# Eight PSUM banks, cut differently: four pairs, or two pairs and four single banks

## The chip, the cores and the metric

The kernel runs on one core of a Trainium2 chip. The metric is device time in microseconds (us), the median of several runs. In the text PE is the matrix engine (TensorE), ACT the activation engine (ScalarE), DVE the vector engine (VectorE), POOL is GpSimd and SP the engine that issues most transfers. PSUM is the memory into which PE writes; ACT and DVE empty it. It has eight banks of 512 float32 values for each of 128 partitions, and one matmul writes into one bank.

## The reference

Eight images of 8 channels and 256 x 256 pixels pass through a grouped Fourier neural operator (4 groups of 2 channels), with a residual, and then through a 3 x 3 dilation with a residual. Everything is float32.

```python
# layer 0, on the normalised x, per group: 2 channels and 2 grid planes -> 10 channels
h = _gconv1x1(h, fc0_w, fc0_b)
for i in range(4):
    h1 = _spectral_conv(h, sp_w1[i], sp_w2[i])   # FFT, 24 x 12 modes kept, mixed, FFT back
    h2 = _gconv1x1(h, w_w[i], w_b[i])
    h = h1 + h2
    if i < 3:
        h = _gswish(h, betas[i])
h = _gswish(_gconv1x1(h, fc1_w, fc1_b), betas[3])   # 10 -> 128 channels per group
x = x + _gconv1x1(h, fc2_w, fc2_b)                  # 128 -> 2 channels per group
# layer 1
x = x + dilate3x3(_gn(x))
```

## The kernel before: the parts concerned

The four Fourier layers of image b ("layers") and the fc1/fc2 part of image b - 1 ("head") are interleaved: the program puts single steps of the head between pieces of the layers. The instructions of PE, ACT and DVE stand in a fixed order that the program gives. The first image's layers have no head beside them, and the last image's head has no layers beside it.

Every PSUM tile comes from one ring of four pairs of banks. A tile that needs only one bank takes a pair and leaves half of it unused. A taker waits until the tile that had its place four takings earlier has been read.

```python
def ps_z(name):
    return ps.tile([128, 2, 512], F32, tag="z", bufs=4, name=name)

def ps_a(name):
    return ps_z(name)[:, 0, :]
```

Four places fill four banks at once, with one matmul per bank from each of four row groups of PE. Two of them, with the copy of the Fourier rows between:

```python
def copy_2(i, dst, src):
    if i % 2:
        nc.scalar.activation(dst, src, AF.Identity)
    else:
        nc.vector.tensor_copy(dst, src)

def turn(c):                       # DVE, after burst(c): two transpositions of h
    # ... for i in range(2): of h[:, c, 2 * i : 2 * i + 2]

def transform(k):                  # rows to frequencies, two chunks of h
    pair = [ps_z(f"p_d_{b}_{l}_{k}_{i}") for i in range(2)]
    for v in range(8):
        for q in range(NQ):
            mm(pair[q // 2][part(v % 4), q % 2, : 240 * n], fw8[part(q), v, :],
               t[part(q), :, :, v, : NBLK * WID], start=v < 4, stop=v >= 4)
    for i in range(2):
        copy_2(i, e[:, 2 * i : 2 * i + 2], pair[i][:, :, : 240 * n])

def gather(k):                     # sums the four parts of a transform, one bank
    p = ps_a(f"p_u_{b}_{l}_{k}")
    # ... four matmuls, a copy to zt by DVE

def burst(c):                      # one chunk of the next h: 1x1 convolution and rows back
    pair = [ps_z(f"p_z_{b}_{l}_{c}_{i}") for i in range(2)]
    for f in range(NQ):
        for q in range(NQ):
            o = pair[q // 2][part(f), q % 2, :]
            # ... mm(o, weights, h[:, c, f], start=True, stop=False)
    for s in range(2):
        for q in range(NQ):
            mm(pair[q // 2][:, q % 2, HW * s : HW * (s + 1)],
               zt[part(q), 2 * c + s].rearrange("p f o -> p (f o)"), binv[part(q), :],
               start=False, stop=s == 1)
    for i in range(2):
        dst = h[:, c, 2 * i : 2 * i + 2, :]
        if l < 3:
            nc.scalar.activation(dst, pair[i], AF.Silu)
        else:
            nc.scalar.activation(dst, pair[i], AF.Identity, bias=bias3)
```

The head has 128 steps an image. Each step calls `first`; each even one calls `second` before it.

```python
def first(n):                      # fc1 of one piece of 512 pixels, four groups
    act = sb.tile([128, G, 512], F32, tag="act", bufs=4, name=f"act_{b}_{n}")
    pair = [ps_z(f"p_fc1_{b}_{n}_{i}") for i in range(2)]
    for g in range(G):
        mm(pair[g // 2][:, g % 2, :], w1[part(g), blk, :], hs[k][part(g), :], start=True, stop=True)
    for i in range(2):
        nc.scalar.activation(act[:, 2 * i : 2 * i + 2, :], pair[i], AF.Silu)

def second(n):                     # fc2 of two pieces, into one bank
    y, acc = box["y"], ps_a(f"p_fc2_{b}_{n}")
    for i in range(2):
        act = acts.pop(n + i)
        for g in range(G):
            mm(acc[part(g), :], w2[:, g, 15 - rb - i : 47 - rb - i], act[:, g, :],
               start=i == 0, stop=i == 1)
    # ... DVE adds acc to y

# the head's loop
if n % 2 == 0 and n > 3:
    second(n - 4)
first(n)
```

Other takers of PSUM: `rows_of` (tile `p_g`, a pair each, five per layer and image, emptied by DVE), the transpositions of x (`p_xt`, a pair each), and single banks for sums, `p_b`, `p_f` and the like. In layers 0 to 2, two chunks of a layer run in the order burst, second, first, transform, burst, gather, first; in layer 3, a chunk is burst, first, second, first.

Of the kernel before, what the change touches and what calls it, by code (L numbers as in the profile page):

```python
# [10 lines left out]
F32 = mybir.dt.float32  # L11
AF = mybir.ActivationFunctionType
# [6 lines left out]
HW = 256  # L19
# [25 lines left out]
def fno_dilate_kernel(ctx: ExitStack, tc: tile.TileContext, a: dict, out: bass.AP):  # L45
    nc = tc.nc
    mm = nc.tensor.matmul
# [4 lines left out]
    ps = ctx.enter_context(tc.tile_pool(name="ps", bufs=2, space=PSUM))  # L52
# [1 line left out]


    def ps_z(name):
        return ps.tile([128, 2, 512], F32, tag="z", bufs=4, name=name)

    def ps_a(name):
        return ps_z(name)[:, 0, :]  # L60

    def part(i):
        return slice(32 * i, 32 * i + 32)
# [10 lines left out]
    def load(name, shape, eng=nc.gpsimd):  # L74
        t = const.tile(list(shape), F32, tag=f"c_{name}", name=f"c_{name}")
        eng.dma_start(t, a[name])
        return t
# [9 lines left out]
    fw8 = load("fw8", (128, 8, 32), nc.sync)  # L87
# [14 lines left out]
    bias3 = load("bias3", (128, 1))  # L102
    w1 = load("w1", (128, NBLK, HID))
# [4 lines left out]
    h = const.tile([128, NCH, NQ, PIX], F32, tag="h", name="h")  # L108
# [41 lines left out]

    wc = const.tile([128, 32], F32, tag="wc", name="wc")
    p = ps_z("p_wc")
    for g in range(G):
        mm(p[32 * g : 32 * g + 6, 0, :32], fc0x[part(g), :], wt[part(g), 0, g, :], start=True, stop=True)
# [40 lines left out]
            nc.vector.tensor_copy(dst, src)  # L195

    def copy_2(i, dst, src):
        if i % 2:
            nc.scalar.activation(dst, src, AF.Identity)  # L199
        else:  # L200
            nc.vector.tensor_copy(dst, src)  # L201
# [23 lines left out]
    def spectrum_x(b, out_):  # L225
# [19 lines left out]
        for half in range(2):  # L245
            xn = x[:, half].rearrange("p (r w) -> p r w", r=8)
            for r in range(0, 8, 4):
# [10 lines left out]
                yield 1.4  # L258
        yield 2
        p = ps_a(f"p_a0_{b}")  # L260
        for f in range(2):
            for q in range(4):
# [85 lines left out]
    def load_sw(l, k):  # L348
        t = sb.tile([128, G, 2 * WID, WID], F32, tag="sw")
        nc.sync.dma_start(t.rearrange("p g m i -> p (g m i)"), a["spw"][l, k])  # L350
        return t
# [72 lines left out]
    def layer(b, l, out_, stored, side):  # L424
        group_in_f = l % 2 == 1

        def turn(c):

            dst = turned[:, c % 3].rearrange("p (s f x) -> p f s x", s=2, f=NQ)
            for i in range(2):  # L430
                nc.vector.transpose(  # L431
                    dst[:, 2 * i : 2 * i + 2], h[:, c, 2 * i : 2 * i + 2].rearrange("p f (s x) -> p f s x", s=2))

        def chunks_of(k):

            return sorted(range(2 * k, min(2 * k + 2, NCH)), key=lambda c: c % 3)

        def transform(k):


            cs = chunks_of(k)
            n, lo = len(cs), cs[0] % 3
            step = cs[-1] % 3 - lo if n == 2 else 1
            t = turned[:, lo : lo + step * (n - 1) + 1 : step].rearrange("p n (r v i) -> p n r v i", r=2 * NQ, v=8)
            pair = [ps_z(f"p_d_{b}_{l}_{k}_{i}") for i in range(2)]
            for v in range(8):
                for q in range(NQ):
                    mm(pair[q // 2][part(v % 4), q % 2, : 240 * n], fw8[part(q), v, :],  # L448
                       t[part(q), :, :, v, : NBLK * WID], start=v < 4, stop=v >= 4)
            e = turned[:, (2 * k + 1) % 3, : 960 * n].rearrange("p (q x) -> p q x", q=NQ)  # L450
            for i in range(2):
                copy_2(i, e[:, 2 * i : 2 * i + 2], pair[i][:, :, : 240 * n])

        def gather(k):

            cs = chunks_of(k)
            n = len(cs)
            e = turned[:, (2 * k + 1) % 3, : 960 * n].rearrange("p (q r f i) -> p q r f i", q=NQ, r=2 * n, f=NQ)
            p = ps_a(f"p_u_{b}_{l}_{k}")
            for g in range(NQ):  # L460
                m = e[:, :, :, g] if group_in_f else e[:, g].rearrange("p q r i -> p r q i")
                mm(p[part(g), : 240 * n], stack, m, start=True, stop=True)  # L462
            src = p[:, : 240 * n].rearrange("p (r g i) -> p r g i", r=2 * n, g=G)
            if cs == sorted(cs):
                nc.vector.tensor_copy(zt[:, 4 * k : 4 * k + 2 * n, :, : NBLK * WID], src)
            else:
                for i, c in enumerate(cs):
                    nc.vector.tensor_copy(zt[:, 2 * c : 2 * c + 2, :, : NBLK * WID], src[:, 2 * i : 2 * i + 2])

        def burst(c):  # L470
            pair = [ps_z(f"p_z_{b}_{l}_{c}_{i}") for i in range(2)]
            for f in range(NQ):
                for q in range(NQ):
                    o = pair[q // 2][part(f), q % 2, :]
                    if l == 0:
                        k = slice(32 * q, 32 * q + 6)
                        mm(o, wcn[k, :], h[k, c, f, :], start=True, stop=False)  # L477
                    else:
                        g = f if group_in_f else q
                        mm(o, wt[part(q), l, g, :], h[part(q), c, f, :], start=True, stop=False)  # L480
            for s in range(2):
                for q in range(NQ):
                    mm(pair[q // 2][:, q % 2, HW * s : HW * (s + 1)],  # L483
                       zt[part(q), 2 * c + s].rearrange("p f o -> p (f o)"), binv[part(q), :],
                       start=False, stop=s == 1)
            for i in range(2):
                dst = h[:, c, 2 * i : 2 * i + 2, :]
                if l < 3:
                    nc.scalar.activation(dst, pair[i], AF.Silu)  # L489
                else:  # L490
                    nc.scalar.activation(dst, pair[i], AF.Identity, bias=bias3)  # L491
            if l == 3:
                nc.sync.dma_start(stored[c], h[:, c].rearrange("p f w -> p (f w)"))

        def read_x(c):
            for g in range(G):
                nc.sync.dma_start(
                    h[32 * g : 32 * g + 6, c].rearrange("p f w -> p (f w)"), a["xp"][b, c, g])

        if l == 0:  # L500
            for c in range(NCH):
                read_x(c)
            wcn = sb.tile([128, 32], F32, tag="wcn", bufs=1, name=f"wcn_{b}")
            nc.vector.tensor_scalar(wcn, wc, out_["mr"][:, 1:2], None, ALU.mult)
        if l == 3:
            room = 0.0
            yield "odd"
            for c in range(NCH):
                burst(c)
                room += SIDE  # L510
                while room > 0.0:
                    room -= next(side, SIDE)
                yield (LAST,)
            return
        yield "even"
        for c in range(NCH):
            k = c // 2
            if c % 2 == 0:
                burst(c)
                yield (1,)  # L520
                turn(c)
                if k > 0:
                    transform(k - 1)
            else:
                burst(c)
                if k > 0:
                    gather(k - 1)
                yield (1,)
                turn(c)
        out_["sw"] = [load_sw(l + 1, 0), load_sw(l + 1, 1)]  # L530
        yield 1
        gather(k - 1)
        transform(k)
        yield 2
        gather(k)
        yield 1
# [71 lines left out]
    def head(b, stored, stats):  # L608
        hs, acts, box = {}, {}, {}
# [12 lines left out]
        def first(n):  # L622

            k, blk = n // 32 * NCH + n % 32 // NBLK, n % 32 % NBLK
            act = sb.tile([128, G, 512], F32, tag="act", bufs=4, name=f"act_{b}_{n}")
            pair = [ps_z(f"p_fc1_{b}_{n}_{i}") for i in range(2)]
            for g in range(G):
                mm(pair[g // 2][:, g % 2, :], w1[part(g), blk, :], hs[k][part(g), :], start=True, stop=True)  # L628
            for i in range(2):
                nc.scalar.activation(act[:, 2 * i : 2 * i + 2, :], pair[i], AF.Silu)  # L630
            acts[n] = act

        def second(n):
# [34 lines left out]
        for n in range(STEPS):  # L668
            if n % 32 % NBLK == 0:
                load_state(n // 32 * NCH + n % 32 // NBLK + 2)  # L670
# [3 lines that stand above are left out]
            yield  # L674
# [249 lines left out]
```

## Time and profile before

Median of three runs: 4047.03 us (4043.34 to 4052.0). The profiled execution has a span of 4041.6 us and a mean granted PE clock of 0.977. Busy shares of some stretches, from the view of busy time by window:

| stretch of the span, us | what runs | PE busy | ACT busy | DVE busy |
|---|---|---|---|---|
| 0 to 386 | layers of the first image alone | 235.04 | 139.38 | 251.12 |
| 850 to 1300 | layers and head interleaved | 435.15 of 450 | 328.40 | 295.33 |
| 1730 to 1809 | mostly layer 3, with head | 73.20 of 79 | 62.36 | 55.57 |
| 3755 to 4018 | head of the last image alone | 245.90 of 263 | 230.96 | 105.74 |

How to read the views: in the table of groups each row is line, engine, operation, what it writes and reads, its shape and count, then busy time and mean nanoseconds, then the engine's idle time before such instructions and who ended it. In the order of time a row is start, length, engine, line, and in brackets the idle time before it with its releaser. PEld is PE's weight load, which stands before each matmul and can run beside an earlier one. Each float32 matmul of the program appears as two loads and two matmuls. The ends of matmuls are modelled, so start times are the safer ground.

### The profile page before, as it was taken

To read this page: it belongs to the slowest core of one execution; us is meant where nothing else is said; L and a number is where in the kernel's file an instruction comes from. 1 tells how busy PE (TensorE), PEld (TensorE's weight loads), DVE (VectorE), ACT (ScalarE), POOL (GpSimd) and SP (SyncE) were. 2 spreads that over 40 slices of the span, in tenths; PEclk is the share of its full clock that TensorE was granted. 3 is DMA by queue.
4 is the path that set the end of the run, shared out by engine and by line. 5 is a ranking of instruction groups with operands and counts; after the bars stand their busy time and mean duration, and the time that the engine had idled before them with its cause. 6 is when DMAs were issued, how large, how long until landed. Compare 5 with 4: busy or idle time off the path is not lost.

```text
span 4041.6 us, 118640 instructions
## 1 busy us (share of the span) xinstructions
PE 3734.7 (92%) x53530; PEld 1463.3 (36%) x53530; DVE 2538.8 (63%) x3535; ACT 2853.1 (71%) x2991; POOL 117.0 (3%) x202
## 2 busy tenths in 40 slices
PE   5666999999999999999999999999999999999997
PEld 2333333433333333333433333333333333333221
DVE  6765656556766666766666666666676666673533
ACT  3334777777777777777777777777777777778886
POOL 1000000000000000000000000000000000000000
PEclk8888999999999999999999999999999999999998
DMA  3005111432125321252122611144121532215311
GB/s 85 14 14 188 53 33 41 139 123 58 58 67 166 93 59 58 82 189 56 55 64 89 197 44 53 53 134 151 55 59 51 164 109 63 61 48 194 96 53 46
DMA packets 113985, 345.05 MB, mean 85 GB/s; under 512 B 15768, under 2 KB 18392, under 8 KB 98056
## 3 DMA queue, kind: packets, MB, share of 16 engines
q1 hardware_dynamic: 95288, 276.33, 22.0%
q0 software_dynamic: 18192, 61.13, 4.7%
q8 instruction: 422, 6.91, 0.7%
q14 instruction: 83, 0.68, 0.1%
HBM read 213.40 MB, written 123.74 MB: 83 GB/s over the span
## 4 chain that ended last, share of the span: by engine, by line
PE 78%; DVE 11%; ACT 7%; issue 3%; DMA 1%; POOL 0%; DVEq 0%; POOLq 0%; SPq 0%; ACTq 0%
PE p_fc L650 22%; PE p_fc L628 20%; PE p_z L483 8%; PE p_z L480 7%; PE p_d L448 6%; ACT act L630 4%; PE p_u L462 3%; PE p_z L477 3%; DVE turned L431 2%; PE p_b L333 2%; PE p_g L405 2%; PE p_g L410 2%; ACT h L491 2%; DVE turned L324 2%; DVE turned L201 1%
## 5 line engine op out<-in xcount | busy, mean ns | idle before, releaser
L630 ACT ACTIVATE act<-p_fc 128x1024 f32<-128x1024 f32 x2048 | 1960.1, 1026 | 669.6 <-PE p_fc L628 665.3
L628 PE MATMUL p_fc<-hs,c_w 32*128 32x512 f32 x8192 | 1204.4, 631 | 14.8 <-DVE turned L195 8.5
L650 PE MATMUL p_fc<-act,c_w 128*32 128x512 f32 x8192 | 997.5, 601 | 47.1 <-ACT act L630 35.5
L628 PEld LDWEIGHTS p_fc<-hs,c_w 32*128 32x128 f32 x8192 | 402.3, 183 | 697.3 <-ACT act L630 278.5
L489 ACT ACTIVATE h<-p_z 128x1024 f32<-128x1024 f32 x528 | 511.7, 1021 | 190.5 <-PE p_z L483 189.8
L431 DVE STREAM_TRANSPOSE turned<-h 128x1024 f32<-128x1024 f32 x528 | 623.2, 1219 | 23.4 <-ACT h L489 23.1
L655 DVE TENSOR_TENSOR y<-p_fc,y 128x512 f32<-128x512 f32 x392 | 270.6, 690 | 497.1 <-PE p_fc L650 496.1
L650 PEld LDWEIGHTS p_fc<-act,c_w 128*32 128x32 f32 x8192 | 227.5, 109 | 645.6 <-issue 345.5
L483 PE MATMUL p_z<-c_binv,zt 32*128 32x256 f32 x5632 | 411.7, 405 | 0.6 <-ACT zt L193 0.6
L480 PE MATMUL p_z<-h,c_wt 32*32 32x512 f32 x8448 | 371.1, 601 | 6.7 <-DVE y L655 3.4
L483 PEld LDWEIGHTS p_z<-c_binv,zt 32*128 32x128 f32 x5632 | 261.6, 186 | 305.4 <-issue 295.8
L448 PE MATMUL p_d<-turned,c_fw 32*32 32x480 f32 (+1 forms) x9216 | 309.9, 540 | 11.1 <-DVE turned L431 11.1
L195 DVE COPY zt<-p_g 128x264 f32<-128x264 f32 x300 | 162.6, 629 | 167.1 <-PE p_g L410 91.6
L491 ACT ACTIVATE h<-p_z,c_bias 128x1024 f32<-128x1024 f32 x176 | 186.5, 1111 | 38.8 <-PE p_z L483 38.4
L199 ACT ACTIVATE turned<-p_d 128x960 f32<-128x960 f32 x144 | 130.1, 903 | 94.5 <-PE p_d L448 94.5
L363 DVE TENSOR_REDUCE S<-turned 128x80 f32<-128x800 f32 x192 | 188.8, 983 | 4.7
L448 PEld LDWEIGHTS p_d<-turned,c_fw 32*32 32x32 f32 x9216 | 121.5, 103 | 187.1 <-issue 150.6
L360 DVE TENSOR_TENSOR turned<-t,B 128x800 f32<-128x800 f32 x192 | 188.6, 982 | 0.9 <-DMA t<-in_spw 0.8
L462 PE MATMUL p_u<-turned,c_stack 128*32 128x480 f32 (+1 forms) x1152 | 137.3, 546 | 42.9 <-DVE turned L201 42.9
L324 DVE STREAM_TRANSPOSE turned<-zt 128x960 f32<-128x960 f32 x96 | 175.6, 1857 | 0.6
L201 DVE COPY turned<-p_d 128x960 f32<-128x960 f32 x144 | 152.1, 1057 | 28.9 <-PE p_d L448 28.7
L480 PEld LDWEIGHTS p_z<-h,c_wt 32*32 32x32 f32 x8448 | 93.7, 103 | 211.2 <-ACT act L630 69.1
(169 smaller groups left out, 1964.8 us busy)
## 6 DMA issues: line engine op xcount, KB each, us to landing
stored<-h SPq DMA_DIRECT2D x88, 1024.0 KB
hs<-stored SPq DMA_DIRECT2D x352, 256.0 KB
t<-in_spw SPq DMA_DIRECT2D x96, 400.0 KB
yin<-y_rows POOLq DMA_DIRECT2D x56, 512.0 KB, 5.0
h<-in_xp SPq DMA_DIRECT2D x352, 48.0 KB
turned<-in_x SPq DMA_DIRECT2D x16, 1024.0 KB
y<-in_x SPq DMA_DIRECT2D x56, 256.0 KB
y_rows<-y POOLq DMA_DIRECT2D x56, 256.0 KB, 2.3
```

The source lines that it names most:

```text
L324: nc.vector.transpose(rows[:, 960 * g : 960 * (g + 1)].rearrange("p (i r) -> p i r", r=32), windows(g))
L431: nc.vector.transpose(dst[:, 2 * i : 2 * i + 2], h[:, c, 2 * i : 2 * i + 2].rearrange("p f (s x) -> p f s x", s=2))
L448: mm(pair[q // 2][part(v % 4), q % 2, : 240 * n], fw8[part(q), v, :], t[part(q), :, :, v, : NBLK * WID], start=v < 4, stop=v >= 4)
L462: mm(p[part(g), : 240 * n], stack, m, start=True, stop=True)
L480: mm(o, wt[part(q), l, g, :], h[part(q), c, f, :], start=True, stop=False)
L483: mm(pair[q // 2][:, q % 2, HW * s : HW * (s + 1)], zt[part(q), 2 * c + s].rearrange("p f o -> p (f o)"), binv[part(q), :], start=False, s ...
L489: nc.scalar.activation(dst, pair[i], AF.Silu)
L491: nc.scalar.activation(dst, pair[i], AF.Identity, bias=bias3)
L628: mm(pair[g // 2][:, g % 2, :], w1[part(g), blk, :], hs[k][part(g), :], start=True, stop=True)
L630: nc.scalar.activation(act[:, 2 * i : 2 * i + 2, :], pair[i], AF.Silu)
L650: mm(acc[part(g), :], w2[:, g, 15 - rb - i : 47 - rb - i], act[:, g, :], start=i == 0, stop=i == 1)
L655: nc.vector.tensor_tensor(y, sums, y, ALU.add)
```

## The change

The eight banks become a ring of two pairs and a ring of four single banks. Whatever fills four banks now takes a single, a pair and a single, and is emptied in three pieces (1, 2 and 1 banks) instead of two. What needs one bank takes one single and no longer a pair. The order of all chains is the same. The aim is that a bank comes free as soon as its own piece has been read, and that no bank lies unused.

```diff
     def ps_z(name):
-        return ps.tile([128, 2, 512], F32, tag="z", bufs=4, name=name)
+        return ps.tile([128, 2, 512], F32, tag="z", bufs=2, name=name)
 
     def ps_a(name):
-        return ps_z(name)[:, 0, :]
+        return ps.tile([128, 512], F32, tag="a", bufs=4, name=name)
+
+    def ps_4(name):
+
+        a, p, b = ps_a(name + "_a"), ps_z(name + "_p"), ps_a(name + "_b")
+        parts = [(0, 1, a.unsqueeze(1)), (1, 2, p), (3, 1, b.unsqueeze(1))]
+        return [a, p[:, 0, :], p[:, 1, :], b], parts
 ...
     def copy_2(i, dst, src):
-        if i % 2:
+        if i == 1:
             nc.scalar.activation(dst, src, AF.Identity)
 ...
         def transform(k):
-            pair = [ps_z(f"p_d_{b}_{l}_{k}_{i}") for i in range(2)]
+            banks, parts = ps_4(f"p_d_{b}_{l}_{k}")
 ...
-                    mm(pair[q // 2][part(v % 4), q % 2, : 240 * n], fw8[part(q), v, :],
+                    mm(banks[q][part(v % 4), : 240 * n], fw8[part(q), v, :],
 ...
-            for i in range(2):
-                copy_2(i, e[:, 2 * i : 2 * i + 2], pair[i][:, :, : 240 * n])
+            for i, m, t in parts:
+                copy_2(i, e[:, i : i + m], t[:, :, : 240 * n])
 ...
         def burst(c):
-            pair = [ps_z(f"p_z_{b}_{l}_{c}_{i}") for i in range(2)]
+            banks, parts = ps_4(f"p_z_{b}_{l}_{c}")
 ...
-            for i in range(2):
-                dst = h[:, c, 2 * i : 2 * i + 2, :]
+            for i, m, t in parts:
+                dst = h[:, c, i : i + m, :]
                 if l < 3:
-                    nc.scalar.activation(dst, pair[i], AF.Silu)
+                    nc.scalar.activation(dst, t, AF.Silu)
                 else:
-                    nc.scalar.activation(dst, pair[i], AF.Identity, bias=bias3)
+                    nc.scalar.activation(dst, t, AF.Identity, bias=bias3)
 ...
         def first(n):
-            pair = [ps_z(f"p_fc1_{b}_{n}_{i}") for i in range(2)]
+            banks, parts = ps_4(f"p_fc1_{b}_{n}")
             for g in range(G):
-                mm(pair[g // 2][:, g % 2, :], w1[part(g), blk, :], hs[k][part(g), :], start=True, stop=True)
+                mm(banks[g], w1[part(g), blk, :], hs[k][part(g), :], start=True, stop=True)
-            for i in range(2):
-                nc.scalar.activation(act[:, 2 * i : 2 * i + 2, :], pair[i], AF.Silu)
+            for i, m, t in parts:
+                nc.scalar.activation(act[:, i : i + m, :], t, AF.Silu)
```

The row tables and the transpositions of x still take pairs, now from a ring of two.

More of the change, by code (lines that the diff above doesn't have):

```diff
@@ L470, in burst @@
         def burst(c):
-            pair = [ps_z(f"p_z_{b}_{l}_{c}_{i}") for i in range(2)]
+            banks, parts = ps_4(f"p_z_{b}_{l}_{c}")
             for f in range(NQ):
                 for q in range(NQ):
-                    o = pair[q // 2][part(f), q % 2, :]
+                    o = banks[q][part(f), :]
                     if l == 0:
@@ L482, in burst @@
                 for q in range(NQ):
-                    mm(pair[q // 2][:, q % 2, HW * s : HW * (s + 1)],
+                    mm(banks[q][:, HW * s : HW * (s + 1)],
                        zt[part(q), 2 * c + s].rearrange("p f o -> p (f o)"), binv[part(q), :],
                        start=False, stop=s == 1)
-            for i in range(2):
-                dst = h[:, c, 2 * i : 2 * i + 2, :]
+            for i, m, t in parts:
+                dst = h[:, c, i : i + m, :]
                 if l < 3:
-                    nc.scalar.activation(dst, pair[i], AF.Silu)
+                    nc.scalar.activation(dst, t, AF.Silu)
                 else:
-                    nc.scalar.activation(dst, pair[i], AF.Identity, bias=bias3)
+                    nc.scalar.activation(dst, t, AF.Identity, bias=bias3)
             if l == 3:
```

## The prediction

> **What bounds the kernel now.** I read the busy times first, then the waits sorted by their sum, then the order of time in four kinds of stretch: heads alone, a layer's chunk pair, the last layer with two head steps a chunk, and the row tables. Short names: f is one `first` (four matmuls into four banks), S one `second` (one bank), z a `burst` and d a `transform` (four banks), g a `gather` (one bank), r a row-table pair (`p_g`).
>
> ```profile
> PE 3734.7 (92%) x53530; PEld 1463.3 (36%) x53530; DVE 2538.8 (63%) x3535; ACT 2853.1 (71%) x2991; POOL 117.0 (3%) x202
> ...
> L630 ACT ACTIVATE act<-p_fc 128x1024 f32<-128x1024 f32 x2048 | 1960.1, 1026 | 669.6 <-PE p_fc L628 665.3
> ...
> L628 PEld LDWEIGHTS p_fc<-hs,c_w 32*128 32x128 f32 x8192 | 402.3, 183 | 697.3 <-ACT act L630 278.5
> ```
>
> PE is the busiest by far and ACT sits idle before `act` because PE has not delivered. But the weight loads of `first`, which must come before its matmuls, wait in turn for ACT to empty banks. So PE is the bound with short holes in it. Which chains do they stand in front of?
>
> ```profile
> PEld p_fc L628 <- ACT act L630: 278.5, 397, 1.4
> PEld p_fc L650 <- ACT act L630: 222.5, 307, 1.4
> PEld p_z L480 <- ACT act L630: 69.1, 129, 1.1
> PEld p_f L379 <- ACT act L630: 25.9, 27, 1.1
> ```
>
> These sums are not lost time: a load issued ahead waits while earlier matmuls still run. The real hole must be read from start times. Heads alone (63 rounds at the end):
>
> ```profile
> 3864.45 0.31 PEld L628 LDWEIGHTS p_fc<-hs,c_w 32*128 32x128 f32 x8 [0.84 <-ACT act L630]
> ...
> 3865.34 0.31 PEld L628 LDWEIGHTS p_fc<-hs,c_w 32*128 32x128 f32 x8 [0.58 <-ACT act L630]
> 3865.68 3.77 ACT L630 ACTIVATE act<-p_fc 128x1024 f32<-128x1024 f32 x4 [0.39 <-PE p_fc L628]
> 3866.76 0.16 PEld L650 LDWEIGHTS p_fc<-act,c_w 128*32 128x32 f32 x8 [1.11 <-ACT act L630]
> ...
> 3868.61 0.31 PEld L628 LDWEIGHTS p_fc<-hs,c_w 32*128 32x128 f32 x8 [0.84 <-ACT act L630]
> ```
>
> A round (f, f, S) is 3868.61-3864.45 = 4.16 us. ACT needs 3.77, PE 0.89+1.07+1.85 = 3.81 (f to f 0.89 here; f to another chain 1.07, as f to d in the layers; S to f 1.85). What sets 4.16 is a loop: ACT starts at 3865.68, frees the first pair 1.03 later, and only then may S start (3866.76), because its accumulator takes the pair that this f had four takings ago. S 1.85, then f to the start of ACT 1.23: 1.08+1.85+1.23 = 4.16.
>
> The last layer (z, f, S, f a chunk) has the same loop through z:
>
> ```profile
> 1741.79 2.12 ACT L491 ACTIVATE h<-p_z,c_bias 128x1024 f32<-128x1024 f32 x2 [0.20 <-PE p_z L483]
> 1742.95 0.16 PEld L650 LDWEIGHTS p_fc<-act,c_w 128*32 128x32 f32 x8 [1.01 <-ACT h L491]
> ...
> 1744.81 0.36 PEld L628 LDWEIGHTS p_fc<-hs,c_w 32*128 32x128 f32 x8 [0.84 <-ACT h L491]
> ...
> 1745.93 0.23 PEld L480 LDWEIGHTS p_z<-h,c_wt 32*32 32x32 f32 x32 [0.76 <-ACT act L630]
> 1746.04 1.94 ACT L630 ACTIVATE act<-p_fc 128x1024 f32<-128x1024 f32 x2 [0.30 <-PE p_fc L628]
> ```
>
> And the row tables, whose tiles stay pairs:
>
> ```profile
> 2075.78 1.63 PEld L405 LDWEIGHTS p_g<-c_rowg,fz 128*128 128x128 f32 x8 [0.76 <-issue]
> ...
> 2075.94 1.94 ACT L630 ACTIVATE act<-p_fc 128x1024 f32<-128x1024 f32 x2 [2.21 <-PE p_fc L628]
> 2076.97 1.98 DVE L195 COPY zt<-p_g 128x264 f32<-128x264 f32 x4 [0.71 <-PE p_g L405]
> 2077.75 0.48 PEld L628 LDWEIGHTS p_fc<-hs,c_w 32*128 32x128 f32 x8 [0.34 <-issue]
> ```
>
> Here two r go down together, right behind an f, and nothing stops them: the four takings before the second r are two older.
>
> **What the Trainium skill says.** "TensorEngine Tiling (Array Packing)", section "Gotcha 1: PSUM Pressure": different row tiles write different banks. So the four matmuls of a chain run side by side and all four banks become full at the same moment; the trace agrees (eight loads within 0.13 us, two passes of four). A finer bank therefore is not filled earlier, only emptied earlier. "PSUM — Partial Sum Buffer", section "Engine vs sequencer instructions": matmuls start and complete in program order. So a chain stands as soon as one of its four banks is taken, and what counts is the last of its releases. "ScalarE: Activation LUTs", section "What ACT_TABLE_LOAD costs": an activation costs 186 ns plus 0.833 ns an element, neighbours overlap by 93 ns. The trace: 960 columns 970 ns, 480 columns 570 ns (0.833 an element, 170 fixed), and activations in a row start 0.92 us apart at 1024, so one more instruction costs ACT some 0.07 us, less than the page's 0.09; for those with a bias the step is 1.00, so 0.15.
>
> **The change part by part.** No matmul is added, removed or moved. (1) ACT gets three instructions in place of two for 1024 f and 352 z. A four-bank chain takes 0.49+0.92+0.49 = 1.91 us instead of 1.84; in all 1288 x 0.07 + 88 x 0.15 = 103 us more ACT (71% to 74%), beside PE. Counted from ACT's start, the first release comes after 0.60 instead of 1.03, the last after 2.01 instead of 1.95. (2) d: ACT keeps one pair, DVE has two copies of 480 (658 ns alone, about 1.23 together by the overlap that two 240-column copies show) instead of one of 960 (1.14): +0.09 us before g may start. (3) S, g and the small chains no longer spend a pair for one bank. (4) The ring order of halves and singles is the same: four singles against four pairs, each chain taking two, S taking one. Only the middle pair has a ring of its own, two deep, shared with r and the transposes.
>
> Round by round, with T the start of ACT on the first f. **f f S:** S may start at T+0.65, so the old loop falls to 0.65+1.85+1.23 = 3.73. A second loop takes over: the second f's first bank is the last bank of the second f before, released at T + 2x1.91 + 0.15 = T + 3.97. From that f to S 1.07, S 1.85, f to ACT 1.23, ACT to the release 3.97: 8.12 for two rounds, 4.06 each. Gain 0.10 to 0.11. There are 63 rounds at the end and about 18 an image in the seven images before, between the layers: 189 x 0.11 = -21 us. **p_f** after f f waits for the same first pair: it starts at 1941.59 where its PE could at 1941.24; with 0.43 earlier release it does: 27 x 0.35 = -9 us. **Layer chunk pair** (z S f d z g f, 11.75 us; unstalled 11.4): d to z waits 0.2 us today for the full release of f, which comes 0.07 later; g waits for DVE's copies in about half the cases, +0.04 on average; f behind g waits up to 0.2 for the first half of z, which ends, but the next z then stands for the full release of the last z (0.1+2.0 us against 2.04 of PE work), so 0.05 is left. Together +0.06 x 110 pairs = +7 us. **Last layer:** S starts as soon as f is through, but the next z needs the last bank of f, which ACT frees after z and f: 2.16+2.01+0.05 = 4.22 after its start; plus z 2.07 and 0.20 to ACT: 6.49 instead of 6.40. Some 77 chunks, of which those slowed by the side work don't feel it: +6 us. **Row tables:** the second r of two needs the middle pair of the f just before. ACT starts that at 2075.94 and frees the middle after 1.41+0.15 = 2077.5; PE was there at about 2076.6. Once in each of 28 layers +0.4 to 0.9, part of it made up behind: +12 us. **First image and first chunks of layers:** the first turning of h needs the pair in the middle (1.5 us after ACT's start instead of 1.0): +5 us. Sum: -30 +30 = 0; I lean a little to the better side, since small chains elsewhere (S between single f, p_u, p_b) find their bank 0.4 us earlier and I counted only those that stand today.
>
> **Rivals.** (a) Waits for the first release are what costs, and all go: by start times f to S stands some 0.5 us in about half of its cases, z and f inside their chains somewhat less; all together I find roughly 180 us of such standing between 400 and 3740 us, and 0.36 a round behind. If half went for good, -100 us, 3945. For it speaks the size of the sums above; against it that in each loop another release of a full chain lies within 0.1 to 0.2 us of the present one, and those get later. (b) ACT becomes the bound: in the last layer ACT works 5.9 of 6.4 us, with the change 6.2, and DVE too has more copies. If each added 0.07 of ACT fell on the path, +103 us, 4150. Against it: ACT is idle before `act` for 669.6 us. (c) The two-deep pair ring hurts more than I think, where DVE is late with the copies of r or of the transposes (DVE runs dilation pieces in between): one further 0.5 us at each of 160 row pairs is +80. For it: DVE copies of one r end just when the next begins.
>
> **Range and chances.** Gains and losses of about 30 us each, none known better than by half: +-20 each; a rival partly right shifts by 40. So 4040 us, 8 in 10 within 3985 to 4090. Two per cent is 81 us; faster than 3966 needs rival (a) to be half right: 0.09; slower than 4128 needs (b) or (c): 0.05; within 0.86.
>
> **What would show it.** ACT busy up by 90 to 130 us with 1376 more activations; rounds at the end of 4.06 us (4.16 or above: the loop is misread; 3.85: no second loop); chunks of the last layer of about 6.5; chunk pairs unchanged within 0.1; a new wait of the second r for `act`; the wait of p_f for `act` nearly gone. I am wrong if rounds fall to PE's 3.8, or if PE's loads wait for copies of r.

## The result and the profile after

The changed kernel takes 4074.55 us (median of 4 runs, 4067.68 to 4077.18) against 4045.59 for the kernel before on the same chip: ratio 1.0066, 95% interval 1.0049 to 1.0084. It is slower by 0.7%. The page of the changed kernel, busy times and groups (busy, mean ns of one, idle time before and its releaser):

```profile
PE 3770.2 (93%) x53530; PEld 1475.4 (36%) x53530; DVE 2552.5 (63%) x3679; ACT 2938.7 (72%) x4367; POOL 117.2 (3%) x202
...
L636 ACT ACTIVATE act<-p_fc_a 128x512 f32<-128x512 f32 x1024 | 621.2, 607 | 608.6 <-PE p_fc_b L634 587.6
L636 ACT ACTIVATE act<-p_fc_p 128x1024 f32<-128x1024 f32 x1024 | 1059.1, 1034 | 1.1
...
L636 ACT ACTIVATE act<-p_fc_b 128x512 f32<-128x512 f32 x1024 | 633.3, 618 | 0.0
...
L634 PEld LDWEIGHTS p_fc_a<-hs,c_w 32*128 32x128 f32 x2048 | 312.8, 183 | 666.8 <-ACT act L636 313.7
```

ACT has 1376 instructions and 85.6 us more, and it still idles before the first pieces (608.6 us in all). PE has the same 53530 matmuls. Most of the waiting of `first` for `act` now shows at its first bank (`p_fc_a`): 313.7 us, and 26.0 more at its other banks, where it was 278.5 in all. These sums do not say where the time went. For that I cut both traces at the starts of PE's chains (first row table, first burst, first `p_b`, first `p_f` of each layer) and added up the stretches. Side work is what the program puts between the chunks of the last layer: the statistics and the transpositions of the next image's x, among others.

| stretch, and how many | before, mean us | after, mean us | all together, us |
|---|---|---|---|
| row tables to the next burst, 32 | 13.7 | 14.9 | +36.8 |
| transpositions of x to `p_f` (last layer with side work; one of the 8 is the first image's start), 8 | 48.8 | 50.0 | +9.0 |
| start of the last layer to the transpositions, 7 | 28.4 | 28.7 | +2.0 |
| `p_f` to row tables, 32 | 5.1 | 5.2 | +2.4 |
| layers 0 to 2, first burst to `p_b`, 24 | 81.6 | 81.2 | -10.4 |
| `p_b` to `p_f`, 24 | 20.1 | 19.8 | -7.9 |
| last image from its last layer on, 1 | 383.3 | 382.8 | -0.5 |

The sum is +31.4 us, the difference of the two spans (4073.0 - 4041.6). So the change wins 18.8 us, nearly all of it from the first burst of layers 0 to 2 to the next `p_f`, and the row tables alone cost about twice that. In layer 2 of an image, f behind a single r, before the change:

```profile
2069.47 0.74 PEld L405 LDWEIGHTS p_g<-c_rowg,fz 128*128 128x128 f32 x4 [0.76 <-issue]
...
2070.55 0.45 PEld L628 LDWEIGHTS p_fc<-hs,c_w 32*128 32x128 f32 x8 [0.34 <-issue]
...
2071.76 0.30 PEld L405 LDWEIGHTS p_g<-c_rowg,fz 128*128 128x128 f32 x2 [0.76 <-ACT act L630]
```

The same place in the changed kernel:

```profile
2089.97 0.74 PEld L411 LDWEIGHTS p_g<-c_rowg,fz 128*128 128x128 f32 x4 [0.76 <-ACT act L636]
...
2090.55 1.02 ACT L636 ACTIVATE act<-p_fc_p 128x1024 f32<-128x1024 f32 x1
2091.05 0.29 PEld L634 LDWEIGHTS p_fc_a<-hs,c_w 32*128 32x128 f32 x2 [0.34 <-ACT act L636]
...
2091.62 0.19 PEld L634 LDWEIGHTS p_fc_p<-hs,c_w 32*128 32x128 f32 x2 [0.27 <-ACT act L636]
...
2092.68 0.74 PEld L411 LDWEIGHTS p_g<-c_rowg,fz 128*128 128x128 f32 x4 [0.76 <-PE p_fc_a L634]
```

The first matmul of this f goes down at 2091.05, and the second only at 2091.62, when ACT has read the middle pair of the f before (2090.55 + 1.02 = 2091.57). Between the two f one r took the other pair. From this r to the next it is 2.71 us, where it was 2.29. Four microseconds on, two r follow each other:

```profile
2095.62 0.18 PEld L634 LDWEIGHTS p_fc_a<-hs,c_w 32*128 32x128 f32 x1 [0.84 <-issue]
...
2096.70 0.74 PEld L411 LDWEIGHTS p_g<-c_rowg,fz 128*128 128x128 f32 x4 [0.76 <-issue]
...
2097.28 1.02 ACT L636 ACTIVATE act<-p_fc_p 128x1024 f32<-128x1024 f32 x1
...
2098.35 0.74 PEld L411 LDWEIGHTS p_g<-c_rowg,fz 128*128 128x128 f32 x4 [0.91 <-ACT act L636]
```

Before the change these two stood as one run of eight loads. Now the second starts at 2098.35, 0.05 us after ACT has read the middle pair (2097.28 + 1.02). Before, its first load stood 0.8 us behind that of the first r (2076.55 behind 2075.78, inside the run of eight); so it could have started at about 2097.5.

Heads alone, where S (L656) to S is a round:

```profile
3984.60 1.92 PE L656 MATMUL p_fc<-act,c_w 128*32 128x512 f32 x16
...
3988.39 0.16 PEld L656 LDWEIGHTS p_fc<-act,c_w 128*32 128x32 f32 x8 [0.76 <-ACT act L636]
...
3990.87 0.64 ACT L636 ACTIVATE act<-p_fc_b 128x512 f32<-128x512 f32 x1
...
3991.57 0.18 PEld L634 LDWEIGHTS p_fc_a<-hs,c_w 32*128 32x128 f32 x1 [1.00 <-ACT act L636]
...
3992.64 0.16 PEld L656 LDWEIGHTS p_fc<-act,c_w 128*32 128x32 f32 x8 [0.76 <-ACT act L636]
```

Rounds are 3.79 and 4.25 in turn, 4.02 on average, where before each was 4.16. In the long one the second f starts at 3991.57, 0.06 after ACT's last piece of the round before (3990.87 + 0.64). This is the loop over two rounds of the prediction. In the last layer:

```profile
3698.99 0.69 ACT L497 ACTIVATE h<-p_z_a,c_bias 128x512 f32<-128x512 f32 x1 [0.41 <-PE p_z_b L489]
...
3699.76 0.16 PEld L656 LDWEIGHTS p_fc<-act,c_w 128*32 128x32 f32 x8 [0.76 <-ACT h L497]
...
3702.52 0.62 ACT L636 ACTIVATE act<-p_fc_b 128x512 f32<-128x512 f32 x1
...
3703.20 0.10 PEld L486 LDWEIGHTS p_z_a<-h,c_wt 32*32 32x32 f32 x1 [1.11 <-ACT act L636]
```

S starts 0.77 after ACT did (1.16 before), but the next burst waits for ACT's last piece of f (3702.52 + 0.62 = 3703.14). Chunks without side work take 6.46 us instead of 6.39.

### The profile page after: what moved, and what is told of

Its sections match the earlier page's. It is cut to its first block, busy times and chain, and to the rows that moved or that the text cites. A ratio compares the mean times of both kernels' runs of the same rounds, so it can differ in the third digit from the quotient of the medians.

```text
span 4073.0 us, 119435 instructions
## 1 busy us (share of the span) xinstructions
PE 3770.2 (93%) x53530; PEld 1475.4 (36%) x53530; DVE 2552.5 (63%) x3679; ACT 2938.7 (72%) x4367; POOL 117.2 (3%) x202
## 4 chain that ended last, share of the span: by engine, by line
PE 68%; ACT 19%; DVE 9%; issue 3%; DMA 2%; POOL 0%; DVEq 0%; SPq 0%; POOLq 0%; ACTq 0%
PE p_fc L656 17%; PE p_fc_a L634 14%; ACT act L636 11%; PE p_z_a L489 8%; PE p_z_a L486 4%; ACT h L497 4%; PE p_d_a L454 3%; ACT h L495 3%; PE p_u L468 2%; PE p_b L339 2%; DVE turned L437 2%; PE p_d_p L454 2%; PE p_z_p L486 2%; PE p_g L416 2%; PE p_g L411 2%
## 5 line engine op out<-in xcount | busy, mean ns | idle before, releaser
L634 PE MATMUL p_fc_b<-hs,c_w 32*128 32x512 f32 x2048 | 1117.8, 633 | 7.4 <-ACT act L636 2.7
L634 PE MATMUL p_fc_a<-hs,c_w 32*128 32x512 f32 x2048 | 1104.8, 630 | 15.8 <-ACT act L636 15.8
L634 PE MATMUL p_fc_p<-hs,c_w 32*128 32x512 f32 x4096 | 1111.1, 630 | 0.0
L636 ACT ACTIVATE act<-p_fc_a 128x512 f32<-128x512 f32 x1024 | 621.2, 607 | 608.6 <-PE p_fc_b L634 587.6
L636 ACT ACTIVATE act<-p_fc_p 128x1024 f32<-128x1024 f32 x1024 | 1059.1, 1034 | 1.1
L656 PE MATMUL p_fc<-act,c_w 128*32 128x512 f32 x8192 | 998.3, 601 | 5.0 <-ACT act L636 4.0
L636 ACT ACTIVATE act<-p_fc_b 128x512 f32<-128x512 f32 x1024 | 633.3, 618 | 0.0
L634 PEld LDWEIGHTS p_fc_a<-hs,c_w 32*128 32x128 f32 x2048 | 312.8, 183 | 666.8 <-ACT act L636 313.7
L656 PEld LDWEIGHTS p_fc<-act,c_w 128*32 128x32 f32 x8192 | 227.4, 109 | 592.6 <-issue 347.1
L489 PE MATMUL p_z_p<-c_binv,zt 32*128 32x256 f32 x2816 | 403.6, 404 | 0.0
L489 PE MATMUL p_z_a<-c_binv,zt 32*128 32x256 f32 x1408 | 401.2, 404 | 0.3 <-ACT zt L199 0.3
L489 PE MATMUL p_z_b<-c_binv,zt 32*128 32x256 f32 x1408 | 401.0, 404 | 0.0
L486 PE MATMUL p_z_a<-h,c_wt 32*32 32x512 f32 x2112 | 361.3, 600 | 14.8 <-ACT act L636 13.0
L634 PEld LDWEIGHTS p_fc_p<-hs,c_w 32*128 32x128 f32 x4096 | 320.3, 183 | 14.3 <-ACT act L636 12.6
L634 PEld LDWEIGHTS p_fc_b<-hs,c_w 32*128 32x128 f32 x2048 | 302.8, 183 | 51.2 <-ACT act L636 13.4
```

What stands on the lines that cost most here:

```text
L489: mm(banks[q][:, HW * s : HW * (s + 1)], zt[part(q), 2 * c + s].rearrange("p f o -> p (f o)"), binv[part(q), :], start=False, stop=s == 1)
L634: mm(banks[g], w1[part(g), blk, :], hs[k][part(g), :], start=True, stop=True)
L636: nc.scalar.activation(act[:, i : i + m, :], t, AF.Silu)
```

## The experiments

In the runs below "the stretch" is the one from the first row table to the next burst. The theory (A): the loss sits in the row tables, and comes from which bank a chain behind a two-bank tile has to wait for. The rival (B): it is the third activation of each chain. In the text "cut" says in which tiles a chain's four banks lie, in the order in which they are taken and emptied: before "pair, pair", changed "single, pair, single". All ratios are against the kernel before, on the same chip, with 95% intervals.

**Every second row table in singles.**

```diff
-            p = ps_z(f"p_g_{b}_{l}_{o}")
+            if o // 2 % 2:
+                p = [ps_a(f"p_g_{b}_{l}_{o}_{u}") for u in range(2)]
+            else:
+                p = ps_z(f"p_g_{b}_{l}_{o}")
+                p = [p[:, u, :] for u in range(2)]
 # ... below, p[u] in place of p[:, u]
```

> The changed kernel, with every second row-table pair (the second and the fourth of five) taking two single banks in place of a pair. Theory A (the loss sits in the row tables, because two row pairs in a row, or row pairs and the middle pair of first, now share a ring of two pairs): the stretch from the first row table to the next burst falls from 14.9 us back to 13.5 to 13.9, 32 times about 1.1, so the time falls by 30 to 38 us against the changed kernel, to 4037 to 4045. Theory B (the loss is the third activation of each chain, which ACT works off in the same stretch): the stretch stays at 14.6 to 15.0 and the time at 4068 to 4078.

Measured: 4057.74 us, ratio 1.0018 (1.0011 to 1.0025). The stretch falls from 14.9 to 14.3 us, about half of the way back. In layer 2 the second of two r is no longer held up: the run of eight loads is whole again, and the next f comes 1.98 us behind its start, as before (2.74 in the changed kernel). But f behind the first r still comes late: the next r starts 2.7 us after the first, as in the changed kernel, against 2.3 before. B is out as what lengthens the stretch, since the third activation is still there; A is right for the double r and leaves the other half open. The time misses the range of A by that half.

**All row tables in singles.**

```diff
-            p = ps_z(f"p_g_{b}_{l}_{o}")
+            p = [ps_a(f"p_g_{b}_{l}_{o}_{u}") for u in range(2)]
 # ... below, p[u] in place of p[:, u]
```

> The changed kernel, with all row tables in two single banks each; the ring of two pairs then belongs to the four-bank chains and the transpositions. Theory A in its narrow form (what counts is which release the fourth row table waits for: here the last bank of the first step just before it, later than its middle pair): the stretch stays at 14.5 to 15.2 us, time 4065 to 4080. Theory A in its wide form (sharing the pairs' ring is what costs, any place outside it will do): 13.5 to 13.9, time 4037 to 4045. Theory B: 14.6 to 15.0, like the changed kernel, so this run tells the two forms of A apart and not A narrow from B.

Measured: 4081.69 us, ratio 1.0078 (1.0065 to 1.009); the stretch is 15.3 us, both a little above the range of A's narrow form and far from the wide one. Taking r out of the pairs' ring does not help by itself; of the two forms of A the narrow one stays. A chain that has a two-bank tile between itself and the chain before it must draw two banks from that chain. In the ring of singles these are its first and its last, and the last comes back after 2.0 us of ACT.

**Every second row table and every second transposition tile of x in singles.** The edit of the first run, and:

```diff
-                t = ps_z(f"p_xt_{b}_{half}_{r}")
+                if r:
+                    t = [ps_a(f"p_xt_{b}_{half}_{r}_{u}") for u in range(2)]
+                else:
+                    t = ps_z(f"p_xt_{b}_{half}_{r}")
+                    t = [t[:, u, :] for u in range(2)]
 # ... below, t[u] in place of t[:, u]
```

> As the run with every second row table in singles, and the second tile of each two transposition tiles of x in two single banks as well. In the changed kernel the second such tile waits 0.97 us for the middle pair of the burst just before. Theory A: the rounds of second, first, burst, transpositions, first fall from 9.93 us to about 9.3, 14 of them in images 1 to 7, so another 7 to 9 us less than with the row tables alone: 4029 to 4037. Theory B: no change against the changed kernel, 4066 to 4078.

Measured: 4049.36 us, ratio 0.9997 (0.9989 to 1.0006). Transpositions to `p_f` takes 49.0 us (48.8 before, 50.0 changed), so 7.7 us less in all, and the time is 8.4 us under the first run: the part of A on the transpositions is right. The time itself lies above the range, by what the row tables still cost (14.4 us a stretch).

**Only the third activation, with the old rings.**

```diff
-            for i in range(2):
-                nc.scalar.activation(act[:, 2 * i : 2 * i + 2, :], pair[i], AF.Silu)
+            for i, m, t in ((0, 1, pair[0][:, 0:1]), (1, 1, pair[0][:, 1:2]), (2, 2, pair[1])):
+                nc.scalar.activation(act[:, i : i + m, :], t, AF.Silu)
 # ... the same in burst
```

> The kernel before, with its ring of four pairs, but the first pair of every first and every burst emptied in two activations of one bank each: only the added instruction of the change (1024 + 352 of them), nothing of its rings. Theory A: row-table stretches as before (13.5 to 13.9 us); rounds of heads alone 4.16 + 0.07 = 4.23, chunks of the last layer 6.39 + 0.07 = 6.46 to 6.55; sum 10 to 30 us over the kernel before, 4056 to 4076. Theory B: row-table stretches 14.5 to 15, time 4080 to 4100.

Measured: 4093.53 us, ratio 1.0102 (1.0089 to 1.0116), about 41 us. The row-table stretch is 13.9 us, so the instruction is not what costs there. Rounds of heads alone are 4.23. But layers 0 to 2 take 82.5 us (81.6 before) and chunks of the last layer 6.60, so the time lies above the range of A and in that of B, though not by B's stretch: one more activation a chain costs more than I had allowed for. That it does so because each release behind it comes later is argued and not shown. The changed kernel does not pay this in full; there the layers take 81.2 us. So the finer rings do win: outside of the row tables the changed kernel takes 5.4 us less than the kernel before, its added instruction included.

**Same rings, other order: cut single, single, pair.**

```diff
-        a, p, b = ps_a(name + "_a"), ps_z(name + "_p"), ps_a(name + "_b")
-        parts = [(0, 1, a.unsqueeze(1)), (1, 2, p), (3, 1, b.unsqueeze(1))]
-        return [a, p[:, 0, :], p[:, 1, :], b], parts
+        a, b, p = ps_a(name + "_a"), ps_a(name + "_b"), ps_z(name + "_p")
+        parts = [(0, 1, a.unsqueeze(1)), (1, 1, b.unsqueeze(1)), (2, 2, p)]
+        return [a, b, p[:, 0, :], p[:, 1, :]], parts
 # and in copy_2: i == 2 in place of i == 1
```

> The changed kernel with the four banks of a chain cut single, single, pair, and emptied in that order; row tables and transpositions stay pairs. Same number of instructions, same sizes of the rings; only the moment at which each ring gets its banks back changes: both singles after 1.1 us of ACT, the middle pair's successor after 2.0 us in place of 1.5. Theory A (a chain that has a two-bank tile between itself and the chain before it needs two of that chain's banks, and what counts is when two of them are back in the ring that it draws on): the pair now comes last, so row-table stretches grow from 14.9 to 15.3 to 16.5 us, time 4085 to 4125. Theory D (how the rings are divided matters, not the order of release): as the changed kernel, 4070 to 4080.

Measured: 4103.58 us, ratio 1.013 (1.0114 to 1.0147); the stretch is 15.8 us. With as many instructions and places as the changed kernel, only the moment of return has moved, and the row tables pay for it. D is out.

**The same cut, with the row tables in singles.** The edit above, all row tables in two singles, and the second of each two transposition tiles in two singles.

> Cut single, single, pair; all row tables in two singles each, and the second of each two transposition tiles too. Theory A: a chain behind a row table draws its two singles from the two that the chain before it gave back after 1.1 us, as the first pair was before the change after 1.03: row-table stretches 13.6 to 14.1 us (14.9 changed, 13.7 before; 15.3 with all row tables in singles and the old cut), rounds of heads alone still in turn 3.79 and 4.24, time 4025 to 4037, faster than the kernel before by 0.3 to 0.6%. Theory D: 15 us and 4065 to 4085, as with all row tables in singles under the old cut.

Measured: 4014.93 us (4010.58 to 4019.37), ratio 0.9913 (0.99 to 0.9927): faster than both kernels, and by more than expected. The stretch is 13.7 us, as before the change, and layers 0 to 2 take 80.9 (81.2 changed, 81.6 before). Of the about 33 us between the spans of this kernel and the one before, layers 0 to 2 give 18.4 and `p_b` to `p_f` 8.3; why the layers gain more than under the changed kernel stays open. The order of time at the same place in layer 2:

```profile
2058.72 0.18 PEld L637 LDWEIGHTS p_fc_a<-hs,c_w 32*128 32x128 f32 x1 [0.84 <-issue]
...
2059.79 1.63 PEld L414 LDWEIGHTS p_g<-c_rowg,fz 128*128 128x128 f32 x8 [0.76 <-DVE y L664]
...
2060.37 0.59 ACT L639 ACTIVATE act<-p_fc_b 128x512 f32<-128x512 f32 x1
...
2061.77 0.18 PEld L637 LDWEIGHTS p_fc_a<-hs,c_w 32*128 32x128 f32 x1 [0.34 <-DVE zt L201]
```

Two r are one run of eight loads again. The second needs both singles of the f at 2058.72; ACT has read them by 2060.96 (2060.37 + 0.59), while the pair still follows. Row tables and chains now fit each other: what wants two banks early finds two that came back early.

**DVE empties a piece of the last layer.** In the changed kernel:

```diff
+                elif i == 3:
+                    nc.vector.tensor_scalar(dst, t, bias3, None, ALU.add)
                 else:
                     nc.scalar.activation(dst, t, AF.Identity, bias=bias3)
```

> The changed kernel, with the last bank of each burst of the last layer (identity plus bias) emptied by DVE in place of ACT. Theory E (a chunk of the last layer is set by ACT, which has to empty the burst and then all of first before the next burst may start): ACT is through about 0.5 us earlier, chunks without side work fall from 6.46 to 5.95 to 6.15 us, time 20 to 30 us under the changed kernel, 4047 to 4057. Theory F (it is set by second, which waits for the burst's first bank, and PE behind it): chunks 6.35 to 6.5, time 4068 to 4078.

Measured: 4117.04 us, ratio 1.0168 (1.0152 to 1.0184). Slower, against both theories. Where no side work runs (last image) E holds nearly as expected: chunks are 6.18 us instead of 6.46. In the other images the side work stands in the way:

```profile
1777.44 0.75 DVE L497 TENSOR_SCALAR h<-p_z_b,c_bias 128x512 f32<-128x512 f32 x1 [1.25 <-PE p_z_b L489]
...
1778.11 2.46 DVE L240 BATCH_NORM_STATS2 bn_x<-turned 128x6 f32<-128x512 f32 x4
...
1782.16 0.68 DVE L663 TENSOR_TENSOR y<-p_fc,y 128x512 f32<-128x512 f32 x1
...
1782.90 0.10 PEld L486 LDWEIGHTS p_z_b<-h,c_wt 32*32 32x32 f32 x1 [1.73 <-DVE y L663]
```

DVE waits 1.25 us for the burst, then does its piece and the statistics of x, and empties S only at 1782.16. The next burst needs that bank, and its loads stand idle for 1.73 us. In the whole run loads of a burst wait 30 times for this addition to y, 47.0 us in all; in the changed kernel it is 6 times and 9.1 us. Transpositions to `p_f` takes 53.9 us (50.0 in the changed kernel).

**Both together.** The cut of the fastest kernel, and the second bank of a burst by DVE.

> Both together: cut single, single, pair; row tables and second transposition tiles in singles; in the last layer the second bank of a burst emptied by DVE. If A and E hold and add up: 20 to 30 us under the run without the DVE part, 3998 to 4015, faster than the kernel before by 0.8 to 1.3%. If E falls or DVE is late with its piece: 4025 to 4040.

Measured: 4054.96 us, ratio 1.0011 (1.0005 to 1.0018). DVE's piece costs about 40 us here as well, with the same signs: chunks without side work 6.18, transpositions to `p_f` 52.4 (48.6 without the piece), and the bursts' waits for the addition to y 46.7 us in 29 cases (11.0 in 11 without it).

**DVE's piece behind the side work.** As the last run, but

```diff
-                burst(c)
+                held = burst(c)
                 room += SIDE
                 while room > 0.0:
                     room -= next(side, SIDE)
+                finish(c, held)     # DVE's piece and the store of the chunk
```

> As the run with both parts (cut single, single, pair; in the last layer the second bank of a burst emptied by DVE), but DVE's piece stands in the order behind the side work that the program puts after a burst, in place of in front of it. Theory G (DVE's piece costs because it stands first and waits for PE, so that the side work and the emptying of second behind it come late): chunks with side work lose their extra time and all come near the 6.18 us of chunks without it; time 10 to 25 us under the run single, single, pair without a DVE piece, 3985 to 4005. Theory H (DVE simply has too much to do in the last layer with 0.7 us more a chunk, wherever it stands): 4040 to 4060, like the run with the piece in front.

Measured: 4037.5 us, ratio 0.9969 (0.9957 to 0.998), between G and H. The first chunks of the last layer, up to the transpositions, fall to 27.4 us (29.8 with the piece in front, 28.6 without it), and the bursts' waits for the addition to y to 13.7 us in 10 cases, as G says; from the transpositions to `p_f` it stays at 52.6, as H says. What part of that is DVE's time and what part its order stays open; without the piece the kernel is faster by 0.6%.

**Only the small tiles changed.** The kernel before, a ring of three pairs and one of two singles:

```diff
-        return ps.tile([128, 2, 512], F32, tag="z", bufs=4, name=name)
+        return ps.tile([128, 2, 512], F32, tag="z", bufs=3, name=name)
-        return ps_z(name)[:, 0, :]
+        return ps.tile([128, 512], F32, tag="a", bufs=2, name=name)
```

> The kernel before with only the small tiles changed: a ring of three pairs and one of two single banks; four-bank chains still take two pairs and are emptied in two activations, small tiles take one single. No bank lies unused. Theory A: the second pair of each chain then always waits for the first pair of the chain just before it, so a round of heads alone becomes 1.08 + 1.07 + 1.85 + 1.23 = 5.23 us, and most chains in the layers stand by some 0.5 to 1 us; time 4400 to 5000. Theory I (what the change gains comes from the small tiles no longer taking a pair): 4000 to 4045.

Measured: 4845.39 us, ratio 1.197 (1.195 to 1.1991). Heads alone:

```profile
4760.81 0.30 PEld L628 LDWEIGHTS p_fc<-hs,c_w 32*128 32x128 f32 x4 [1.15 <-ACT act L630]
...
4761.87 0.16 PEld L650 LDWEIGHTS p_fc<-act,c_w 128*32 128x32 f32 x8 [0.76 <-issue]
...
4767.09 0.16 PEld L650 LDWEIGHTS p_fc<-act,c_w 128*32 128x32 f32 x8 [0.76 <-issue]
```

The second pair of the second f goes down only at 4760.81, after 1.15 us of idle weight loads, when ACT has read the first pair of the f just before. A round is 4767.09 - 4761.87 = 5.22 us, and 5.23 was worked out from the releases. An unused bank is cheap beside a lost place for a chain. Small tiles in singles, paid for with one pair, do not give the gain of the fastest kernel; with eight banks that took a finer cut of the chains as well.

## Why the prediction was right or wrong

The time lies in the range, and "within 2%" came true. The lean was on the wrong side: 4040 was said, 4074.55 came. That it was no further off is partly luck: the row tables cost 22 us more than their term said, and the layers, put at +7 us, gave 14.2. By its steps:

- **ACT.** 103 us of added work were expected, 85.6 came. Expected to lie beside PE's work; with the old rings the added instruction costs some 41 us, so in part it does lie on the path.
- **f f S.** Right in mechanism and nearly in size: 4.06 expected, 4.02 measured, with the second loop that was named. But 189 rounds were counted and there are 162, and of the -21 us -13.4 came: -12.6 from the 98 rounds between the layers and only -0.8 from the 64 at the end. Some rounds became longer: in one that went from 4.45 to 5.69, DVE had stood 4.32 us for a transfer and emptied S late, and the last bank of an f waited 1.61 for it.
- **p_f** (-9 us): wrong. Its wait for `act` was to be nearly gone; it is 24.6 us in 27 waits, before 25.9 in 27. Only in the 14 behind f f was ACT the last to come; in the other 13 `p_f` waited for its operand F from DVE (F ended 0.12 us before it, the named `act` 0.2 to 0.3). In half of the 14 the second f is now held up by the second loop: it starts 1.32 us after its forerunner in place of 0.89, and `p_f` comes 4.25 us after S in place of 4.16. In the other half the f's are free, but `p_f` comes only 0.13 us earlier behind the second f (1.29 in place of 1.42; 0.35 was expected), since now F is the last to come. Two steps of the prediction met here, each worked out as if the other did not exist, and the operand was not looked at.
- **Layer chunk pair** (+0.06, +7 us): from the fifth chunk on a pair takes 11.71 us, as before. But layers 0 to 2 of the seven images with heads became 14.2 us shorter in all, half of it between their third and fifth burst (13.06 us in place of 13.41). So the sign was wrong; what shortens the beginning of the layers stays open.
- **Last layer** (6.49 from 6.40): right, 6.46 from 6.39. The prediction said that side work hides it; instead the 12 steady rounds with transpositions (S, f, burst, transpositions, f) grew from 9.29 to 9.93, since their second tile waits for the burst's middle pair, as the second r does. The mechanism was named for r and not looked for there: +7.8 us.
- **Row tables** (+12 us): this is the term that was mis-sized. The 28 layers that it counted came to +34.4, or 1.23 us each; the four of the first image add 2.4. The wait of the second r was seen and put at 0.4 to 0.9 us, of which I wrote off a part. In layer 2 it delays the f behind it by 0.76. The other wait, of f behind a single r (0.42 us), was not seen. Of these 1.2 us 0.3 is made up before the next burst. The prediction looked at r's own place in the pairs' ring, and not at what r takes from the chain behind it.
- **First image and first chunks** (+5 us): the first image alone costs 8.1 us more up to its last layer.
- **Rivals.** (a), that the early releases win much, is out for this cut and partly right for the fastest one (-0.9%). (b) is partly right by the run with the old rings. (c), in the form that DVE's copies of r hold up the pairs' ring, did not show: PE's second r waits for `act`, and no weight load of the changed kernel waits for DVE's copies of r. Where ACT copies r too, in the first image, loads of r waited 8 times for it, 4.0 us in all. That the two-deep ring of pairs hurts more than thought was right.

## What to carry to other kernels

When a buffer is cut into several rings, draw for every taker which earlier tile it replaces, and note when that one is given back; the number of places does not tell it. What comes between two large chains takes places that the next chain must then draw from its forerunner, so cut a chain such that as many places as the tile in between needs come back together and first. Waits found in this way must be followed round the loop together: a release that comes earlier is worth nothing where another of the same chain decides, and a piece moved to an idle engine can cost more than it saves if it waits there in front of other work.

## What the runs showed of the hardware that was not expected

One more activation in a chain of 2048 columns, from the same banks, costs ACT some 0.06 us of busy time (85.6 us over 1376 instructions), and still 41 us of 4050 in run time under the old rings. Otherwise nothing: from the releases read in the kernel before (a round of heads alone of 4.16 us) the rounds under three other arrangements of the banks were worked out ahead as 4.06, 4.23 and 5.23 us, and came as 4.02, 4.23 and 5.22.
